# A four-layer graph network on one core: half of layer 1 by Strassen's method, its projection summed in PSUM, and some copies moved from VectorE to ScalarE

## The chip, the cores and the metric

The kernel runs on one core of a Trainium2 chip. A core has a matrix engine (TensorE, "PE" in the profile, its weight loads "PEld"), VectorE ("DVE"), ScalarE ("ACT"), GpSimd ("POOL") and SyncE ("SP"), which here issues all DMAs, in one queue and in order. The metric is the time of one execution on the device, in microseconds (us); less is better.

## The reference, cut to what matters

Four attention layers over one graph of 3327 nodes with 256 features each. Every layer adds its result to its input and normalises the sum over the features. The layer that the change touches is layer 1, a graph attention layer:

```python
h = x @ W                              # 256 -> 256
e = (h @ a[:D])[:, None] + (h @ a[D:])[None, :]
e = leaky_relu(e, 0.01)
attention = softmax(where(adj > 0, e, MASK_VAL), axis=1)
h_prime = attention @ h
x = layernorm(x + elu(h_prime))
```

Layer 0 is attention by cosine similarity, layer 2 scaled dot-product attention with learned q, k and v, and layer 3 consists of three graph attention layers like layer 1 (called 3a, 3b and 3c).

## The kernel before, in words

**Tiles and blocks.** The nodes are padded to 26 tiles of 128. The queries are taken in 7 blocks of 512 (four tiles; the last block has two tiles, 256 queries). A layer is 7 blocks by 26 steps: step (b, j) multiplies the weights of key tile j for the queries of block b with the values of tile j, and sums over j in PSUM. All of it is f32.

**One step of layer 1.** `Gat.weights` (L785) makes one tile of weights e, 128 keys by 512 queries: ScalarE computes re (L788), VectorE adds, and multiplies by the mask (L801). TensorE then multiplies e, 128 queries at a time, with V of tile j, which has 256 features and a column of ones that gives the softmax's sum: four matmuls of 257 columns (L1687). Weights are made three steps ahead in the program; the pool "e" has nine buffers, and the engines run ahead as far as buffers allow.

**Strassen's method.** Layers 0 (blocks 1 to 5), 2, 3a, 3b and 3c take a pair of key tiles and pairs of query tiles as a 2x2 by 2x2 product of blocks, in seven products in place of eight (L940: matmuls of 128 columns, or 129 with the column of ones). For that VectorE makes sums of e (L884 to L887, or L872 to L875 for four tiles of layer 3 at once). The sums of V, "tsums", are made once per pair of key tiles by `combine` (L845 to L853), stored to DRAM (L854, t_d) and fetched again for every block and pair (L858, 256.5 KB each, three buffers). Layer 1 in this kernel is plain.

**The end of a block.** `finish` (L1102) is a generator that moves on by one piece per step while the next block runs. In layer 1 it takes the reciprocal of the softmax's sums (L1198, L1201), normalises on ScalarE into p (L1186), splits p into upper and lower 16 bits ("planes", L994, ScalarE), transposes by DMA (L997, "turned"), copies the two halves to pT (L1004, VectorE), and multiplies with the layer's W. For blocks 0 to 4 this projection is done by Strassen as well, in `projected4`: sums of pT ("psums", L1043 to L1046), seven products of two matmuls each into fresh places of PSUM (L1058), one copy on ScalarE (L1071) and seven additions on VectorE (L1072 to L1082). Then come elu, the addition of x (L1258, L1267), the statistics (L1114, L1115) and the last step of the layernorm, o (L1296, VectorE); o is stored (L1308), and is split, transposed and copied once more (ft, L1004) to be projected to layer 2's values (pv, L1326, v at L1333), keys' sums (ksum, L630 to L633) and tsums.

**What sets the order.** The program is written step by step; a tile scheduler then fixes each engine's own order, in which the engine runs, waiting where its next instruction must wait. Masks (1664 KB per block of four tiles, two buffers) are fetched by `fetch_mask` (L427), u, the query side of the weights, at L775.

The functions that the diff touches:

Of the kernel before, what the change touches and what calls it, by code (L numbers as in the profile page):

```python
# [33 lines left out]
def gnn_stack(ctx: ExitStack, tc: tile.TileContext, a: dict, N: int, out: bass.AP):  # L34
# [31 lines left out]
    def bank(name):  # L66
        return ps_b.tile([P, CH], F32, tag="pb", name=name)
# [25 lines left out]
    for k in range(4):  # L93
# [18 lines left out]

    t_d = {
        k: [dram.tile([P, 4 * H + 1], F32, name=f"t{k}_d{p}") for p in range(NT // 2)]
        for k in ("0", "2", "3a", "3b", "3c")
    }
    x_d = {
        k: [dram.tile([P, D], F32, name=f"x{k}_d{t}") for t in range(NT)]
# [697 lines left out]
    def strassen(L, b):  # L816
# [3 lines left out]
            return b < NB - 1  # L820
        return L.key == "2"

    def deep(L):
        return L.i > 2

# [5 lines left out]
    def combine(key, p, v, e=None):  # L831


        b1, b2 = v[2 * p], v[2 * p + 1]
        b11, b12, b21, b22 = b1[:, H:D], b1[:, :H], b2[:, H:D], b2[:, :H]
        if (key, p) in kept or key == "0":
            t = work.tile([P, 4 * H + 1], F32, tag="tsum", name="tsums", bufs=3)
        else:
            t = work.tile([P, 4 * H + 1], F32, tag="x4k", name="tsum", bufs=2)
        if (key, p) in kept:  # L840
            tsums[kept[key, p], p] = t
        t1, t2, t3, t4 = (t[:, c : c + H] for c in (0, H + 1, 2 * H + 1, 3 * H + 1))
        if e is None:
            nc.gpsimd.memset(t[:, H : H + 1], 1.0)
            nc.vector.tensor_tensor(t1, b12, b11, ALU.subtract)  # L845
            nc.vector.tensor_tensor(t3, b22, b12, ALU.subtract)
        else:
            one = t[:, H : H + 1]
            nc.vector.tensor_scalar(one, e[:, :1], 0.0, None, ALU.is_ge)
            nc.vector.scalar_tensor_tensor(t1, b12, one, b11, ALU.mult, ALU.subtract)  # L850
            nc.vector.scalar_tensor_tensor(t3, b22, one, b12, ALU.mult, ALU.subtract)
        nc.vector.tensor_tensor(t2, b22, t1, ALU.subtract)
        nc.vector.tensor_tensor(t4, t2, b21, ALU.subtract)  # L853
        nc.sync.dma_start(t_d[key][p], t)  # L854
# [23 lines left out]
    def sums(b, e1, e2):  # L878

        hw = bw(b) // 2  # L880
        s3, s1, s2, s4 = (x[:, i, :hw] for x in two_slots("ssum") for i in range(2))
        e11, e21 = e1[:, :hw], e1[:, hw : 2 * hw]
        e12, e22 = e2[:, :hw], e2[:, hw : 2 * hw]
        nc.vector.tensor_tensor(s3, e11, e21, ALU.subtract)  # L884
        nc.vector.tensor_tensor(s1, e21, e22, ALU.add)
        nc.vector.tensor_tensor(s2, s1, e11, ALU.subtract)  # L886
        nc.vector.tensor_tensor(s4, e12, s2, ALU.subtract)  # L887
        return e11, e12, e22, s1, s2, s3, s4

    def places(pos, b):  # L890

# [95 lines left out]
    def turn(x4, n, out, steps=3, copy=nc.vector.tensor_copy):  # L987

        half = "p k (n t) -> p t k n"
        pl = work.tile([P, 4, 2, D], U16, tag="x4k", name="planes", bufs=2)
        for t in range(2):
            nc.scalar.copy(pl[:, :n, t, :], x4[:, :n, :].bitcast(U16).rearrange(half, t=2)[:, t])  # L994
        yield
        tr = work.tile([P, 16, P], U16, tag="stage", name="turned", bufs=4)
        nc.sync.dma_start_transpose(  # L997
            out=tr[:, : 4 * n, :], in_=pl[:, :n].rearrange("p k t n -> p (k t n)")
        )
        for _ in range(steps):  # L1000
            yield
        trv = tr[:, : 4 * n, :].rearrange("p (k t h) i -> p t k h i", t=2, h=2)
        for t in range(2):
            copy(out(t), trv[:, t])  # L1004
        yield

    def early(L, b):
# [17 lines left out]
    def sum_weights(wt):  # L1025
        b11, b12, b21, b22 = (wt[:, h, o * H : (o + 1) * H] for h in range(2) for o in range(2))
        t1, t2, t3, t4 = wsum
        nc.vector.tensor_tensor(t1, b12, b11, ALU.subtract)
        nc.vector.tensor_tensor(t3, b22, b12, ALU.subtract)
        nc.vector.tensor_tensor(t2, b22, t1, ALU.subtract)  # L1030
        nc.vector.tensor_tensor(t4, t2, b21, ALU.subtract)

    def projected4(pT4, wt, c4):

# [15 lines left out]
        cv = c4.rearrange("p (a k) (o f) -> p a k o f", k=2, o=2)  # L1050
        c11, c12, c21, c22 = (cv[:, :, k, o, :] for k in range(2) for o in range(2))

        def two(*pairs):

            pm = bank("pproj")
            for i, (l, r) in enumerate(pairs):
                for k in range(2):
                    nc.tensor.matmul(  # L1058
                        pm[:, (2 * i + k) * P : (2 * i + k + 1) * P],
                        l[:, k, :],  # L1060
                        r,
                        start=True,
                        stop=True,
                    )
            v = pm.rearrange("p (i a f) -> p i a f", i=2, a=2)
            return v[:, 0], v[:, 1]

        m1, m2 = two((a11, b11), (a12, b21))
        m6, m7 = two((s2, t2), (s3, t3))
        yield  # L1070
        nc.scalar.copy(c22, m1)  # L1071
        nc.vector.tensor_tensor(c11, c22, m2, add)  # L1072
        nc.vector.tensor_tensor(c22, c22, m6, add)
        nc.vector.tensor_tensor(c21, c22, m7, add)
        m5, m4 = two((s1, t1), (a22, t4))
        yield
        nc.vector.tensor_tensor(c12, c22, m5, add)
        nc.vector.tensor_tensor(c22, c21, m5, add)
        nc.vector.tensor_tensor(c21, c21, m4, sub)
        m3, _ = two((s4, b22))  # L1080
        yield
        nc.vector.tensor_tensor(c12, c12, m3, add)  # L1082

    class Sum:

# [16 lines left out]
    def finish(L, b, pos):  # L1102
# [76 lines left out]
        else:  # L1179
# [9 lines left out]
            if strassen(L, b):  # L1189
                z, L.joined = joined(pos, b, p4)  # L1190
                nc.vector.tensor_scalar(z, z, TINY, None, ALU.max)
                nc.vector.reciprocal(z, z)
                for k in range(n):
                    normed(p4[:, k, :], p4[:, k, :], z[:, k : k + 1])
            else:
                for k, t in enumerate(ts_):
                    ri = cols.tile([P, 1], F32, tag="ri", name="ri", bufs=4)
                    nc.vector.tensor_scalar(  # L1198
                        ri, pos[k][:, D : D + 1], TINY, None, ALU.max
                    )  # L1200
                    nc.vector.reciprocal(ri, ri)  # L1201
                    normed(p4[:, k, :], pos[k][:, :D], ri)
            if L.key in x_d:
                x4 = work.tile([P, 4, D], F32, tag="stage", name="x4", bufs=4)
                xr = [x4[:, k, :] for k in range(4)]
# [7 lines left out]
            if L.key != "2":  # L1213
# [5 lines left out]
                        "p k h (i t) -> p t k h i", t=2  # L1219
                    )[:, t],  # L1220
                    turn_steps(L, b),
                    nc.scalar.copy if early(L, b) else nc.vector.tensor_copy,
                )
                if early(L, b):
                    yield
                    yield
                pTs = {k: pT4[:, k] for k in range(n)}
                if L.key == "1" and b < NB - 2:
# [55 lines left out]
        if not L.hidden:  # L1284
# [7 lines left out]
                dsts = [o4[:, k, :] for k in range(n)]  # L1292
            else:
                dsts = [nxt[t][:, :D] for t in ts_]
            for k, t in enumerate(ts_):
                nc.vector.tensor_scalar(  # L1296
                    dsts[k],
                    ys[k],
                    st[:, k, 0:1],
                    r[:, k : k + 1],  # L1300
                    ALU.subtract,
                    ALU.mult,
                )
                if L.key == "3c":
                    q = LASTP if t == NT - 1 else P
                    nc.sync.dma_start(out[t * P : t * P + q, :], dsts[k][:q])
# [7 lines left out]
            if L.key == "1":  # L1314
# [4 lines left out]
                        "p h (k i t) -> p t k h i", k=4, t=2  # L1319
                    )[:, t, :n],  # L1320
                    4 if b == NB - 2 else 3,
                )
                for k, t in enumerate(ts_):
                    pm = bank("pv")
# [35 lines left out]
        if b == NB - 1:  # L1360
# [2 lines left out]
                L.sum.add(t, x)  # L1363
            yield
            L.sum.close(nxt[NT - 1])
            if L.i:
                yield
                combine(layers[L.i + 1].key, NT // 2 - 1, nxt)
            if L.gat_next is not None:
# [151 lines left out]
        return j < NT - 2 and (b > 0 or j > 3)  # L1521

    def make_weights(L, b, j, es=None):
        if strassen(L, b) and j % 2 == 0 and kept.get((L.key, j // 2)) != b:
            fetch_tsum(L.key, b, j // 2)
        if by_pairs(L, b, j // 2):
            if j % 2 == 0:
# [3 lines left out]
        else:  # L1531
            if L.is_gat:
                made.append(L.gat.weights(b, j))
                if deep(L) and strassen(L, b) and in_quad(b, j):
                    made[-1] = cells.setdefault((L.i, b, j // 2), []) if j % 2 else None
                    if j % 4 == 3:
# [54 lines left out]
    for s, (L, b, j) in enumerate(steps):  # L1591
# [6 lines left out]
        if j == 0:  # L1598
            wo, no = (CH, 4) if strassen(L, b) else (D + 1, len(tiles_of(b)))
            pos = [  # L1600
                ps_o.tile([P, wo], F32, tag="po", name="po") for _ in range(3 if end else no)
            ]
        if first:

# [42 lines left out]
        if end:  # L1647
# [33 lines left out]
                ends.append(finish_last(pos[0], xm, 0))  # L1681
            if ends:
                next(ends[0], None)
        elif not strassen(L, b):
            todo = [(es, j, k) for k in range(len(pos))]
            for e, i, k in todo:
                nc.tensor.matmul(  # L1687
                    pos[k],
                    e[:, k * P : (k + 1) * P],
                    V[L.i % 2][i],  # L1690
                    start=(i == 0),
                    stop=(i == NT - 1),
                )
        elif j % 2:
            products(pos, b, j // 2, es, V[L.i % 2], between if L.key == "2" else None)
        if s == 3:
# [29 lines left out]
        begin = 14  # L1726
        if deep(L) and b < NB - 1:
            begin = 2 if last and b == NB - 2 else 10
        if L.key == "1" and (b, j) == (0, 22):
            sum_weights(w[L.w])  # L1730
        if L.key == "2" and b * NT + j in KSTEPS:
# [96 lines left out]
```

## Time and profile before

| | us |
|---|---|
| median of 3 runs | 2264.83 (2264.76 to 2266.15) |
| profiled execution | 2266.49 |
| its span in the profile | 2264.7 |
| TensorE busy | 2235.8 |
| VectorE busy | 1973.7 |
| ScalarE busy | 1320.0 |
| layer 1: start of its first product to the first of layer 2 | 467.6 to 808.3 |

A row of a group in the profile is: line, engine, operation, out<-in, shapes, count | busy time in us, mean ns of one | idle time of the engine just ahead of them in us, and what ended most of it. A row of a stretch is start:end and length, then busy time and number of instructions for PE, PEld, DVE, ACT and POOL, the granted TensorE clock, the DMA share and GB/s. A row of a timeline is start, duration, engine, line, operation, and in brackets the idle time before it with what ended it. The granted clock is 1.00 in all stretches that are read here.

By the starts of their first matmuls the blocks of layer 1 begin at 467.6, 513.5, 565.3, 617.2, 670.2, 722.1 and 773.9 us.

### The profile page before, as it was taken

The numbers are of one execution on the slowest core, as the hardware profiler recorded it, in microseconds if no ns is written. First come the engines' busy times: TensorE is split into PE (matmuls) and PEld (weight loads), VectorE is DVE, ScalarE is ACT, GpSimd is POOL, SyncE is SP. The second block draws the span as 40 slices with busy tenths as digits, with TensorE's granted clock in tenths as the row PEclk, the third lists the DMA queues.
The fourth block names the chain that finished last, engine by engine and source line by source line (L and its number), as shares of the span: only waits on it lengthen the run. The fifth ranks groups of instructions, "written<-read, shape, count | busy, mean of one in ns | idle before, by whom it ended". The sixth has DMA issues, their size and how long they took to land. (4 is left out here: it accounts for less than half of the span.)

```text
span 2264.7 us, 42094 instructions
## 1 busy us (share of the span) xinstructions
PE 2235.8 (99%) x15333; PEld 2027.7 (90%) x15333; DVE 1973.7 (87%) x5386; ACT 1320.0 (58%) x2259; POOL 42.3 (2%) x196
## 2 busy tenths in 40 slices
PE   9999999999999999999999999999999999999997
PEld 7788887888888879999999998999999999999997
DVE  6789999967677778988998879999899999899997
ACT  4677777765545534444444445666666765665663
POOL 0000001000000000000000000000000000000000
PEclk9999999999999999999999999999999999999999
DMA  8655655522322232232232244545435545355542
GB/s 277 198 179 169 194 193 191 175 90 72 87 82 56 68 87 82 62 96 88 61 96 73 74 146 144 147 137 151 130 112 155 143 131 152 103 159 167 152 121 56
DMA packets 186210, 286.16 MB, mean 126 GB/s; under 512 B 80413, under 2 KB 105492, under 8 KB 181396
## 3 DMA queue, kind: packets, MB, share of 16 engines
q1 hardware_dynamic: 185732, 283.22, 42.3%
q8 instruction: 121, 1.98, 0.4%
q14 instruction: 85, 0.70, 0.1%
q10 hardware_dynamic: 272, 0.26, 0.0%
HBM read 228.21 MB, written 38.44 MB: 118 GB/s over the span
## 5 line engine op out<-in xcount | busy, mean ns | idle before, releaser
L788 ACT ACTIVATE re<-u,nrh,th 128x512 f32<-128x512 f32 (+1 forms) x728 | 531.8, 776 | 291.3 <-DVE e L801 146.7
L1687 PE MATMUL po<-v,e 128*128 128x257 f32 x1872 | 422.6, 381 | 1.2 <-ACT p L1186 1.1
L1687 PEld LDWEIGHTS po<-v,e 128*128 128x128 f32 x1872 | 352.6, 190 | 61.1 <-issue 9.8
L940 PE MATMUL po<-tsums,qsum 128*128 128x128 f32 (+1 forms) x2520 | 351.7, 275 | 5.8 <-DMA tsums<-t3a_d 3.0
L801 DVE SCALAR_TENSOR_TENSOR ft<-re,rh,mask 128x512 f32<-128x512 f32 x468 | 337.5, 742 | 3.2 <-ACT re L788 3.2
L940 PEld LDWEIGHTS po<-tsums,qsum 128*128 128x128 f32 x2520 | 315.4, 192 | 7.8 <-issue 2.8
L940 PE MATMUL po<-tsums,ssum 128*128 128x128 f32 (+1 forms) x2082 | 316.7, 275 | 2.1 <-DVE ssum L886 1.0
L940 PEld LDWEIGHTS po<-tsums,ssum 128*128 128x128 f32 x2082 | 286.6, 192 | 16.9 <-issue 5.0
L940 PE MATMUL po<-v,ft 128*128 128x129 f32 x1872 | 286.3, 276 | 0.9 <-DVE ft L801 0.5
L940 PEld LDWEIGHTS po<-v,ft 128*128 128x128 f32 x1872 | 251.8, 192 | 5.7 <-DVE ft L801 1.1
L940 PEld LDWEIGHTS po<-v,e 128*128 128x128 f32 x1196 | 170.2, 191 | 35.9 <-issue 23.9
L524 ACT ACTIVATE ex<-ps,rq 128x512 f32<-128x512 f32 (+1 forms) x183 | 118.9, 652 | 114.9 <-PE ps L511 111.9
L940 PE MATMUL po<-v,e 128*128 128x129 f32 x1196 | 183.3, 275 | 0.0
L801 DVE SCALAR_TENSOR_TENSOR e<-re,rh,mask 128x512 f32<-128x512 f32 (+1 forms) x234 | 148.2, 655 | 34.5 <-PE po L1687 24.3
L496 DVE SCALAR_TENSOR_TENSOR e<-ex,mask 128x512 f32<-128x512 f32 (+1 forms) x182 | 118.1, 649 | 61.9 <-ACT ex L673 30.8
L511 PE MATMUL ps<-ft 128*128 128x512 f32 (+1 forms) x364 | 166.9, 564 | 0.0
L525 DVE SCALAR_TENSOR_TENSOR e<-ex,mask 128x512 f32<-128x512 f32 (+1 forms) x183 | 116.6, 643 | 33.4 <-ACT ex L524 33.0
L940 PE MATMUL po<-tsums,ft 128*128 128x128 f32 x936 | 143.3, 275 | 0.1
L940 PE MATMUL po<-v,qsum 128*128 128x128 f32 x840 | 128.2, 275 | 0.0
L940 PEld LDWEIGHTS po<-tsums,ft 128*128 128x128 f32 x936 | 123.5, 192 | 0.4 <-ACT p L1186 0.3
L467 DVE CUSTOM_DVE_ANT_0 acc<-acc,stage 128x1024 uint16<-128x1024 uint16 (+1 forms) x168 | 108.5, 646 | 11.3 <-DMA stage<-in_adj_a 8.2
L650 PE MATMUL ps<-gsums,ksum 128*128 128x256 f32 x408 | 111.3, 380 | 0.0
(347 smaller groups left out, 3639.5 us busy)
## 6 DMA issues: line engine op xcount, KB each, us to landing
mask<-mask_d SPq DMA_DIRECT2D x30, 1664.0 KB
stage<-in_adj_a SPq DMA_DIRECT2D x78, 512.0 KB
tsums<-t_d SPq DMA_DIRECT2D x152, 256.5 KB
tsums<-t3a_d SPq DMA_DIRECT2D x77, 256.5 KB
tsums<-t3b_d SPq DMA_DIRECT2D x77, 256.5 KB
tsums<-t3c_d SPq DMA_DIRECT2D x77, 256.5 KB
mask_d<-mask SPq DMA_DIRECT2D x6, 1664.0 KB
u<-s_d SPq DMA_DIRECT2D x24, 256.0 KB
```

What stands on the lines that cost most here:

```text
L467: nc.vector.tensor_tensor(acc, acc, st[:, h * wd : (h + 1) * wd], ALU.add)
L496: nc.vector.scalar_tensor_tensor(e[:, :wd], t_[:, :wd], 0.0, mask(b, j), ALU.add, ALU.mult)
L511: nc.tensor.matmul(ps[:, :wd], FT[j // 4][:, 0, (j % 4) * P : (j % 4 + 1) * P], FT[b][:, 1, :wd], start=True, stop=True,)
L524: nc.scalar.activation(t_[:, c], ps[:, c], AF.Exp, scale=rq[:, j : j + 1])
L525: nc.vector.scalar_tensor_tensor(e[:, c], t_[:, c], 0.0, mask(b, j)[:, c], ALU.add, ALU.mult)
L650: nc.tensor.matmul(out, l, r, start=first, stop=True, skip_group_check=True)
L788: nc.scalar.activation(t_[:, :wd], self.u[b][:, :wd], AF.Relu, bias=self.nrh[:, j : j + 1], scale=self.th[:, j : j + 1],)
L801: nc.vector.scalar_tensor_tensor(e[:, :wd], t_[:, :wd], self.rh[:, j : j + 1], mask(b, j), ALU.add, ALU.mult,)
L940: nc.tensor.matmul(o, x, y, start=(p == 0 and g not in banks[:i]), stop=(p == NT // 2 - 1 and g not in banks[i + 1 :]),)
L1687: nc.tensor.matmul(pos[k], e[:, k * P : (k + 1) * P], V[L.i % 2][i], start=(i == 0), stop=(i == NT - 1),)
```

## The change

1. In layer 1, blocks 1 to 6, the first two query tiles of a block are multiplied by Strassen's method and the other two plainly; block 6, which has only two, entirely by Strassen. `half_sums` makes four 128x128 sums per pair of key tiles (L901 to L904 after the change), `half_products` the seven products, `half_joined` puts them together at the block's end (L953 to L963). Layer 1 gets tsums of its own: `combine("1", p)` for 13 pairs, seven of them during layer 0's last block, and the fetches.
2. `projected4` adds products in PSUM, by further matmuls into the same place: four copies on ScalarE and three additions on VectorE, where it was one and seven. The number of matmuls stays. For that the sign of one sum of W is turned.
3. In blocks 0 to 4 of layer 1 (`eased`) both copies to pT and one of the two copies to ft go to ScalarE, and the last step of the layernorm as well, for which VectorE makes one small array nm.

By the fixed order of each engine, the number of matmuls of 257 columns falls by 312 and that of 128 or 129 columns rises by 546; VectorE gets 356 instructions more, ScalarE 56 more, SyncE 91 more. From layer 2's start on the order is as before. A cut of the diff:

```diff
+    def half(L, b):
+        return L.key == "1" and b > 0
+    def eased(L, b):
+        return L.key == "1" and b < NB - 2
...
+    def half_sums(e1, e2):
+        x = work.tile([P, 4, P], F32, tag="e", name="hsum", bufs=9)
+        s3, s1, s2, s4 = (x[:, i, :] for i in range(4))
+        e11, e21 = e1[:, :P], e1[:, P : 2 * P]
+        e12, e22 = e2[:, :P], e2[:, P : 2 * P]
+        nc.vector.tensor_tensor(s3, e11, e21, ALU.subtract)
+        nc.vector.tensor_tensor(s1, e21, e22, ALU.add)
+        nc.vector.tensor_tensor(s2, s1, e11, ALU.subtract)
+        nc.vector.tensor_tensor(s4, e12, s2, ALU.subtract)
+        return e11, e12, e22, s1, s2, s3, s4
...
+    def half_products(pos, b, p, es, v, ks):
...
+        for k in ks:
+            g, c, n = HALF[k]
+            nc.tensor.matmul(
+                pos[g][:, c : c + n],
+                *m[k],
+                start=(p == 0 and k in (1, 7)),
+                stop=(p == NT // 2 - 1 and k in (5, 3)),
+            )
+    def half_joined(pos, c):
...
+        nc.scalar.copy(c22, m(1))
+        v = pos[-2][:, : 3 * (H + 1)].rearrange("p (s n) -> p s n", n=H + 1)
+        nc.vector.tensor_copy(z[:, :2], v[:, 0::2, H])
+        nc.vector.tensor_tensor(z[:, :1], z[:, :1], v[:, 1, H:], add)
+        nc.vector.tensor_tensor(c11, c22, m(2), add)
+        nc.vector.tensor_tensor(c22, c22, m(6), add)
+        nc.vector.tensor_tensor(c21, c22, m(7), add)
+        nc.vector.tensor_tensor(c12, c22, m(5), add)
+        nc.vector.tensor_tensor(c22, c21, m(5), add)
+        nc.vector.tensor_tensor(c21, c21, m(4), sub)
+        nc.vector.tensor_tensor(c12, c12, m(3), add)
...
         for t in range(2):
-            copy(out(t), trv[:, t])
+            (copy[t] if isinstance(copy, tuple) else copy)(out(t), trv[:, t])
...
+        pm = bank("pproj")
+        r, m2 = pm[:, :D], pm[:, D:]
+        put(r, a11, b11, first=True)
+        put(m2, a12, b21)
+        yield
+        nc.scalar.copy(c11, both(r))
+        nc.vector.tensor_tensor(c11, c11, both(m2), add)
+        put(r, s2, t2)
+        yield
+        nc.scalar.copy(c12, both(r))
+        put(r, s3, t3)
+        q = bank("pproj")[:, :D]
+        put(q, s1, t1, first=True)
+        yield
+        nc.scalar.copy(c22, both(r))
+        nc.vector.tensor_tensor(c22, c22, both(q), add)
+        put(r, a22, t4)
+        put(q, s4, b22)
+        yield
+        nc.scalar.copy(c21, both(r))
+        nc.vector.tensor_tensor(c12, c12, both(q), add)
...
+                if eased(L, b):
+                    nc.scalar.activation(
+                        dsts[k], ys[k], AF.Identity, bias=nm[:, k : k + 1], scale=r[:, k : k + 1]
+                    )
...
-        if strassen(L, b) and j % 2 == 0 and kept.get((L.key, j // 2)) != b:
+        if (strassen(L, b) or half(L, b)) and j % 2 == 0 and kept.get((L.key, j // 2)) != b:
             fetch_tsum(L.key, b, j // 2)
...
+                if half(L, b) and j % 2:
+                    made[-1] = made[-1], half_sums(made[-2], made[-1])
...
+        elif half(L, b):
+            v = V[L.i % 2]
+            if j % 2 == 0:
+                plain(pos[:-2], es, j, v, 2)
+                if j == 2:
+                    half_products(pos, b, 0, held, v, (7, 6, 4, 3))
+            else:
+                plain(pos[:-2], es[0], j, v, 2)
+                held = es[1]
+                half_products(pos, b, j // 2, held, v, (1, 2, 5) if j == 1 else (1, 2, 5, 7, 6, 4, 3))
...
+        if L.key == "0" and b == NB - 1 and j % 3 == 0 and 0 < j < 22:
+            combine("1", j // 3 - 1, V[1])
+        if L.key == "1" and b == 0 and j % 3 == 1 and j < 15:
+            combine("1", 7 + j // 3, V[1])
```

## The prediction

> **What bounds the kernel now.** I read the busy shares first, then the groups, then the stretches, then single stretches of VectorE and SyncE. From the page:
>
> ```profile
> span 2264.7 us, 42094 instructions
> PE 2235.8 (99%) x15333; PEld 2027.7 (90%) x15333; DVE 1973.7 (87%) x5386; ACT 1320.0 (58%) x2259; POOL 42.3 (2%) x196
> L1687 PE MATMUL po<-v,e 128*128 128x257 f32 x1872 | 422.6, 381 | 1.2 <-ACT p L1186 1.1
> L940 PE MATMUL po<-tsums,ssum 128*128 128x128 f32 (+1 forms) x2082 | 316.7, 275 | 2.1 <-DVE ssum L886 1.0
> ```
>
> TensorE (PE) is busy nearly all the time. Its busy time is per row modelled, so I price a matmul by what is spent per record: 422.6/1872 = 226 ns for a 128x257 record of layer 1; in the trace such records start 217 ns apart, and the 128x128 and 128x129 records of layer 0 start 112 ns apart. An f32 matmul is two records: 434 and 224 ns. "1.2 <-ACT" says that the plain matmuls wait for nothing worth naming: layer 1 is bound by PE.
>
> Next the stretches (columns: start:end, length, then busy time and count of PE, weight loads, VectorE (DVE), ScalarE (ACT), GpSimd, then granted clock, DMA share, GB/s):
>
> ```profile
> 300.00:460.00 160.00, 159.57 (x1025) 130.78 (x1024) 149.93 (x447) 118.37 (x191) 10.18 (x27) 1.00 0.55 174
> 512.50:564.00 51.50, 51.50 (x252) 45.28 (x251) 37.60 (x100) 27.24 (x40) 1.23 (x2) 1.00 0.29 75
> 564.00:615.00 51.00, 51.00 (x249) 44.83 (x249) 35.72 (x93) 26.84 (x40) 0.77 (x2) 1.00 0.33 88
> 615.00:666.00 51.00, 49.93 (x244) 43.85 (x244) 37.87 (x102) 26.84 (x40) 1.31 (x2) 1.00 0.29 84
> 666.00:718.00 52.00, 52.00 (x255) 45.70 (x254) 37.71 (x97) 27.11 (x41) 1.32 (x2) 1.00 0.23 61
> ```
>
> The first row is layer 0, where Strassen runs already: VectorE is at 94% and PE still doesn't starve. The others are about one block of layer 1 each (51.9 us by the starts of the blocks). VectorE has 37 us of work in 52, but it doesn't rest at will: it is an in-order engine, and its idle time is made of two waits per block. This is the first of them:
>
> ```profile
> 565.74 0.17 DVE L1201 RECIPROCAL ri<-ri 128x1 f32<-128x1 f32 x1
> 575.51 1.38 DVE L1004 COPY pT<-turned 128x1024 uint16<-128x1024 uint16 x2 [9.61 <-DMA turned<-planes]
> ...
> 579.13 3.40 DVE L801 SCALAR_TENSOR_TENSOR e<-re,rh,mask 128x512 f32<-128x512 f32 x5
> ```
>
> All of VectorE stands for 9.61 us (7.5 in the other blocks) while ScalarE normalises and splits, and the DMA transposes. It costs nothing today: the weights e are up to eight tiles ahead. The second wait, ahead of the ft copies, is 2.6 to 4.2 us.
>
> **PE's part of the change.** For two key tiles, two query tiles cost 4 x 434 = 1736 ns plainly and 7 x 224 = 1568 by Strassen. 168 ns for each of 13 pairs, in 6 blocks: 13.1 us less, 2.18 per block. The projection's 14 matmuls stay.
>
> The Trainium skill, "TensorE: Matmul & The Clock Gate", section "Back-to-back issue gap", speaks against the change: it has sustained spacings of 81 ns at 128 columns and 131 at 512, the narrow matmul paying for its weight load. If 257 columns cost what lies between (some 98), 14 narrow passes would cost more than 8 wide ones, and PE would lose. The trace's 112 against 217 decides: here narrow ones are nearly in proportion.
>
> **VectorE's part, per block.** Added: four 128x128 sums per pair, L901 to L904. The same operations for ksum (L630 to L633) start 0.20 to 0.26 apart, 0.89 for four, so 13 x 0.89 = 11.6 us. The joining of seven products, seven adds of 0.25 and four small ones of 0.15, less four small ones for two tiles that need no reciprocal of their own (0.18 each): +1.7. Moved away: two pT copies (1.38 together), one ft copy (0.66), four layernorm steps (0.32 each, 1.3), four of seven projection adds (0.45 each, 1.8), against a small nm (0.15): -5.0. Net +8.3: 37.2 + 8.3 = 45.5 us for blocks 2 to 5, against 49.7 of PE. By work alone VectorE fits, at 92%.
>
> ScalarE gets two copies of the 1.35 us kind (its pT copies in layer 3 take that), a copy of ft, four steps of 0.4 and some small ones, 7 us on 27 of 52: no bound, but a link in the chain below.
>
> **The waits, which the work hides.** In the changed kernel's static order I counted what VectorE can do inside each wait.
> 1. From the last join (L963) the way is: normalise two tiles (0.8), planes (2.0: "567.01 1.99" before), transpose (4.4 alone; 6.5 from the end of planes to the copy at 575.5), two copies, now on ScalarE, one after the other (2.6), then psums on VectorE: 9.8 to 11.9. Between them VectorE's queue holds three e (0.66), half sums and ksum, 4.2 us. The wait is 5.6 to 7.7; I take 6.0. It stands ahead of e of tile 9, which everything later queues behind.
> 2. SyncE's queue. Before, the transpose of o went out ahead of the fetch of the next mask; now the order is tsums, mask (which waits for VectorE's e of tile 25), then that transpose. The trace of before has this order once:
>
> ```profile
> 798.16 0.32 SPq L427 DMA_DIRECT2D mask<-mask_d  x1
> 798.71 7.03 SPq L997 DMA_TRANSPOSE turned<-planes  x1
> ```
>
> and the copy of that transpose starts at 807.78: 9.6 us after the mask's issue. VectorE has five half sums, e of four tiles, two more groups of half sums, the small ones and e of tile 4 to do meanwhile, 7.0 us. The wait is 2.6 us; it would be 0 if the transpose took its lone 5 us. The 7.03 us that SyncE is held also delay three tsums fetches of the next block.
>
> The cycle of VectorE is thus 45.5 + 6.0 + 2.6 = 54.1 us, against 51.9 before and the 49.7 that PE would allow. The cover has shrunk too: e and half sums share nine buffers, three per pair, so the lead is six tiles instead of nine, and a wait of 6 us is no longer swallowed whole.
>
> **The sum**, against the profiled execution (2266.5, of which 2264.7 span; the median of the runs is 1.7 below it). Blocks 2 to 5: three at +2.2, one +0.6 since its mask is half as large: +7. Block 1 has half sums but starts with a lead from block 0, and PE's 2.2 less shows: -2. Block 6 isn't eased, and has 256 queries: a pair costs VectorE two e of 0.41 and 0.89, 1.7 us, against 1.57 of PE; with the same join and waits 38 to 40 us for 34.3: +4.5. Layer 0's last block gets the sums of V for layer 1 (12 of the 13 combines, by VectorE's fixed order; 0.83 each, 10 us) where VectorE has about 10 us free between 425 and 467: 0 to 3, I take +1.5. At layer 2's start, V of the last tiles comes later by the longer chain: +1.5. 13 t_d stores and 78 fetches of 256.5 KB: the DMA share in these stretches is 0.23 to 0.33 and layer 0 runs at 0.55, nothing. Sum +12.5: 2279 profiled, 2277 as a median.
>
> Both ends: waits at 7.7 and 4 with block 6 at 42 give +22, or 2287. With the first wait at 4 and the second gone, each block is PE's or nearly so.
>
> **Rivals.**
> - *Faster.* VectorE keeps up as at 94% in layer 0, for the waits fall inside the lead: its cycle is below 49.7 if the two together are under 4.2 us. Then the five four-tile blocks gain 2.2 each, 11 in all, and block 6 and layer 0 give back 1 to 3: 2266.5 - 9 = 2257.5, 2256 as a median, at best 2252. For it speaks the row of layer 0, where VectorE has waits too and PE none; against it the 9.61 and the order of SyncE.
>
> The Trainium skill is on this side: "Perfetto Trace Analysis", section "Identifying the Most-Contended Engine", ranks engines by occupancy, and by that PE at 49.7 stays ahead of VectorE at 45.5 and the change would bring its whole 13 us. The 9.61 us in which VectorE stood with work behind it is why I don't count it so.
> - *No change.* The waits together are 4.2 to 7, the cycle 50 to 52.5: blocks 1 to 5 gain 0 to 5, block 6, layer 0 and layer 2's start take it back: 2261 to 2269.
> - *It doesn't do what it says.* Excluded for PE: the listing has 312 fewer wide and 546 more narrow matmuls, 135.4 - 122.3 = 13.1 us.
>
> **Numbers.** Forecast, VectorE's chain bounds layer 1: 0.60, 2270 to 2288, likeliest 2277. Faster: 0.27, around 2256. No change: 0.13. The range reaches down into the faster rival, 2254, and up to 2287. 0.2%, about what a measurement of this kernel tells from no change, is 4.5 us: the bounds are 2260.3 and 2269.4.
>
> **What would show it.** Right: in blocks 2 to 5 gaps of PE of 2 to 4 us per block put down to hsum (L903, L904) or e, block starts 53 to 55 us apart, a VectorE gap of some 6 us ahead of psums L1119 and one of 2 to 4 ahead of ft L1080, SyncE held at the transpose behind the mask. Wrong: no gaps of PE above 0.5 us and blocks of 49.7, with VectorE's idle only before buffers of e. Layers 2 to 3c must be unchanged to 1 us, since their instructions keep their order. I would be wrong if the transpose passes the mask, if the half sums are cheaper than 0.89, or if the lead at the block's end is more than I count.

## The result and the profile after

| | us |
|---|---|
| before, median of 4 runs | 2264.97 (2264.76 to 2266.15) |
| changed, median of 4 runs | 2286.11 (2282.14 to 2289.16) |
| ratio | 1.0093, 95% interval 1.008 to 1.0105 |
| profiled execution of the changed kernel, its span | 2289.16, 2287.2 |

The change costs 21 us. 2277 was forecast. The page of the changed kernel:

```profile
span 2287.2 us, 43671 instructions
PE 2234.1 (98%) x15801; PEld 2036.5 (89%) x15801; DVE 2026.0 (89%) x5742; ACT 1359.6 (59%) x2315; POOL 41.9 (2%) x209
L914 PE MATMUL po<-v,e 128*128 128x257 f32 x1248 | 295.3, 381 | 0.6 <-DVE e L525 0.4
```

The plain group has lost its third (1872 to 1248 records), and TensorE's total is hardly lower, 2235.8 to 2234.1: a matmul's busy time lasts longer where the clock is low, and that hides part of what was saved. The stretches of layer 1 tell more (columns as before: PE, PEld, DVE, ACT, POOL, clock, DMA share, GB/s):

```profile
564.00:615.00 51.00, 47.77 (x302) 43.54 (x303) 41.44 (x138) 31.64 (x46) 0.70 (x2) 0.97 0.43 125
615.00:666.00 51.00, 47.29 (x311) 43.20 (x311) 41.54 (x143) 31.84 (x48) 0.77 (x2) 1.00 0.51 127
666.00:718.00 52.00, 46.09 (x282) 41.38 (x281) 38.01 (x127) 28.36 (x42) 0.76 (x2) 0.93 0.49 121
```

Before, TensorE was idle in none of these but one; now it is for 3 to 6 us of each. VectorE is at 73 to 81%, so it isn't simply full. And the granted clock is below 1 in two of the three. What TensorE waited for in layer 1 (TensorE's waits from 468 to 829 us: total, times, longest):

```profile
PE pv L1428 <- ACT ft L1080: 10.7, 4, 3.4
PE pproj L1131 <- ACT pT L1080: 6.1, 4, 2.6
PE po L937 <- DMA tsums<-t_d: 3.4, 2, 2.8
PE po L937 <- DVE pT L1080: 1.6, 1, 1.6
PE pproj L1131 <- DVE c L1149: 1.2, 1, 1.2
PE po L937 <- DVE hsum L903: 0.5, 1, 0.5
```

The same view of before has two rows, 1.1 and 0.7 us. Of the new ones, the half sums have half a microsecond. TensorE waits at the finish's own matmuls: at pv, for the ft copy, and at the projection, for the pT copies, both now on ScalarE. The largest case, in TensorE's timeline:

```profile
672.95 1.47 PE L914 MATMUL po<-v,e 128*128 128x257 f32 x6
677.59 6.67 PE L1428 MATMUL pv<-w_l_wvt,ft 128*128 128x256 f32 x16 [3.17 <-ACT ft L1080]
```

3.17 us of standing still, and then 16 records in 6.67 us, 417 ns each, where such records start 216 ns apart at full clock. The clock says why; these two stretches end where it changed:

```profile
673.35:676.76 3.41, 1.07 (x5) 0.58 (x4) 0.56 (x1) 0.78 (x2) 0.45 (x1) 1.00 1.13 304
676.76:683.59 6.83, 6.00 (x14) 4.84 (x15) 4.66 (x20) 1.59 (x2) 0.22 (x1) 0.50 0.06 23
```

And on SyncE's queue, ahead of that wait:

```profile
664.64 0.32 SPq L427 DMA_DIRECT2D mask<-mask_d  x1
665.67 7.68 SPq L1073 DMA_TRANSPOSE turned<-planes  x1
673.47 1.76 SPq L864 DMA_DIRECT2D tsums<-t_d  x3
```

The transpose is held behind the mask for 7.68 us, and the three tsums of the next block behind the transpose. VectorE's two waits are there too:

```profile
676.20 0.74 DVE L1080 COPY ft<-turned 128x1024 uint16<-128x1024 uint16 x1 [3.15 <-DMA turned<-planes]
698.73 0.43 DVE L1119 TENSOR_TENSOR psums<-pT 128x256 f32<-128x256 f32 x1 [6.87 <-ACT pT L1080]
```

But VectorE also waits for TensorE, to write e where TensorE has still to read (VectorE's waits from 468 to 829 us):

```profile
DVE e L801 <- PE po L914: 11.1, 13, 1.4
DVE e L801 <- PE po L937: 5.0, 10, 1.5
```

**An account of layer 1**, worked out from the starts of TensorE's records between layer 1's first matmul and layer 2's first product: the sum of the full-clock spacings (217, 112 or 216 ns by width), then every excess of over 0.25 us as a wait, then the smaller excesses, among them what the low clock costs.

| kernel (profiled execution) | length | at full clock | waits | smaller excesses |
|---|---|---|---|---|
| before | 340.7 | 337.6 | 2.3 | 0.8 |
| changed | 360.6 | 324.5 | 27.3 | 8.9 |

(The profiled execution of the changed kernel is the slowest of its four.) 13.1 us are saved, to the tenth; 25.0 of waits and 8.1 of smaller excesses are added. Of the latter the low clock has at most 6.8: TensorE had half the clock for 13.7 us of layer 1 (567.53 to 570.95, 676.76 to 683.59, 734.79 to 738.20). 19.9 of the 22.5 us between the spans are this, 1.2 come before layer 1 and 1.2 after layer 2's start.

### The profile page after: what moved, and what is told of

Its sections match the earlier page's. It is cut to its first block, busy times and chain, and to the rows that moved or that the text cites. A ratio compares the mean times of both kernels' runs of the same rounds, so it can differ in the third digit from the quotient of the medians.

```text
span 2287.2 us, 43671 instructions
## 1 busy us (share of the span) xinstructions
PE 2234.1 (98%) x15801; PEld 2036.5 (89%) x15801; DVE 2026.0 (89%) x5742; ACT 1359.6 (59%) x2315; POOL 41.9 (2%) x209
## 5 line engine op out<-in xcount | busy, mean ns | idle before, releaser
L914 PE MATMUL po<-v,e 128*128 128x257 f32 x1248 | 295.3, 381 | 0.6 <-DVE e L525 0.4
L914 PEld LDWEIGHTS po<-v,e 128*128 128x128 f32 x1248 | 229.3, 190 | 40.2 <-issue 7.9
L1016 PEld LDWEIGHTS po<-v,e 128*128 128x128 f32 x1196 | 170.2, 191 | 36.1 <-issue 23.4
L801 DVE SCALAR_TENSOR_TENSOR e<-re,rh,mask 128x512 f32<-128x512 f32 (+1 forms) x234 | 151.2, 655 | 28.7 <-PE po L914 11.1
L496 DVE SCALAR_TENSOR_TENSOR e<-ex,mask 128x512 f32<-128x512 f32 (+1 forms) x182 | 118.1, 649 | 54.9 <-ACT ex L673 30.3
L467 DVE CUSTOM_DVE_ANT_0 acc<-acc,stage 128x1024 uint16<-128x1024 uint16 (+1 forms) x168 | 108.3, 645 | 12.7 <-DMA stage<-in_adj_a 10.9
```

The costliest lines, as they stand in the source:

```text
L467: nc.vector.tensor_tensor(acc, acc, st[:, h * wd : (h + 1) * wd], ALU.add)
L496: nc.vector.scalar_tensor_tensor(e[:, :wd], t_[:, :wd], 0.0, mask(b, j), ALU.add, ALU.mult)
L801: nc.vector.scalar_tensor_tensor(e[:, :wd], t_[:, :wd], self.rh[:, j : j + 1], mask(b, j), ALU.add, ALU.mult,)
L914: nc.tensor.matmul(pos[k - k0], e[:, k * P : (k + 1) * P], v[i], start=(i == 0), stop=(i == NT - 1),)
L1016: nc.tensor.matmul(o, x, y, start=(p == 0 and g not in banks[:i]), stop=(p == NT // 2 - 1 and g not in banks[i + 1 :]),)
```

## The experiments

All times are medians of runs beside runs of the kernel before on the same chip (2264.4 to 2265.8); differences are against that. Theory A: SyncE's order (mask ahead of the transpose) and the waits behind it. Theory B: VectorE has too much work. Theory C, formed after the third run: the moves to ScalarE and the sums in PSUM cost by themselves.

| run | us | against before | ratio, 95% |
|---|---|---|---|
| changed kernel | 2286.1 | +21.1 | 1.008 to 1.0105 |
| 1 mask behind the transpose | 2276.4 | +10.9 | 1.0028 to 1.0059 |
| 2 one half sum of four | 2282.3 | +16.8 | 1.0054 to 1.0087 |
| 3 plain, with the moves and PSUM | 2289.2 | +23.7 | 1.0079 to 1.0125 |
| 4 block 6 plain | 2295.1 | +29.6 | 1.0116 to 1.0161 |
| 5 Strassen's half alone | 2268.8 | +3.6 | 1.0009 to 1.0028 |
| 6 half, and PSUM | 2269.1 | +3.9 | 1.0009 to 1.0028 |
| 7 PSUM alone | 2282.7 | +17.5 | 1.0066 to 1.0096 |
| 8 the moves alone | 2279.1 | +13.8 | 1.0048 to 1.0082 |
| 9 mask behind, pT back on VectorE | 2273.1 | +8.7 | 1.0023 to 1.0049 |
| 10 half, PSUM, projection later | 2268.0 | +3.6 | 1.0004 to 1.0022 |
| 11 half alone, pT and ft later | 2271.1 | +6.7 | 1.0017 to 1.0042 |
| 12 as 10, one half sum of four | 2262.8 | -3.0 | 0.9978 to 0.9997 |

**1. The mask behind the transpose.**

```diff
-            masks[nb] = fetch_mask(nb)
+            if L.key == "1" and ft_turned[0] is not None:
+                with tc.issue_after(ft_turned[0].ins):
+                    masks[nb] = fetch_mask(nb)
```

> The changed kernel, with one difference: in layer 1 the fetch of the next mask is queued on SyncE behind the transpose of o that ends in ft, where the changed kernel has it ahead. Theory A (SyncE's order): the changed kernel's 1.7 to 3.6 us gaps of TensorE ahead of pv, one per block, come from that transpose being behind 1.66 MB of mask, and so does the lowered clock after them; here they fall below 1 us and the time by 10 to 15 us, to 2270 to 2276. Theory B (VectorE has too much work in a block, wherever the mask stands): the gaps move to hsum, and the time stays within 4 us of the changed kernel's 2286.

10 us come back, as A has it: half of the loss. TensorE's waits at pv shrink from 10.7 to

```profile
PE pv L1432 <- ACT ft L1083: 4.1, 3, 2.3
PE pproj L1134 <- DVE c L1152: 3.7, 4, 1.3
PE pproj L1134 <- ACT pT L1083: 2.4, 2, 2.2
```

with 2.2 and 0.6 in two further rows for pv. They don't fall below 1 us each, which A had expected; that the copies on ScalarE hold them up here too is a reading, not tried in this run. B isn't supported; hsum has 0.6 us.

**2. One half sum of four.**

```diff
-        nc.vector.tensor_tensor(s3, e11, e21, ALU.subtract)
         nc.vector.tensor_tensor(s1, e21, e22, ALU.add)
-        nc.vector.tensor_tensor(s2, s1, e11, ALU.subtract)
-        nc.vector.tensor_tensor(s4, e12, s2, ALU.subtract)
-        return e11, e12, e22, s1, s2, s3, s4
+        return e11, e12, e22, s1, s1, s1, s1
```

> The changed kernel with three of the four half sums per pair left out (only s1 = e21 + e22 is made, and it stands for the other three in the products, so layer 1's result is another): 8.7 us less work for VectorE per block, the same matmuls. Theory B (VectorE's work is the cause): the time falls below the kernel before, to 2250 to 2256, with no gap of TensorE left in layer 1. Theory A (SyncE's order): gaps ahead of pv of 1 to 3 us stay in blocks where the mask still goes ahead of the transpose, and only block 6 and part of the rest is won: 2262 to 2272.

4 us for 52 us less work of VectorE (8.7 in each of six blocks), far from the 2250 to 2256 of B; A's 2262 to 2272 was too low as well. The waits at pv fall (10.7 to 7.1 us), those at the projection for pT stay (6.1 and 6.9). The 4 us understate what the cut does in layer 1: in the profiled executions it takes 349.6 us in place of 360.6, and 5 of these 11 us are lost behind it, since TensorE waits 4.7 us for the first tsums of layer 2, which SyncE holds behind a transpose (6.61 us) behind the mask. So VectorE's work has a part in the changed kernel's loss, but B falls as its main cause.

**3. Plain matmuls, with the moves and the sums in PSUM.**

```diff
     def half(L, b):
-        return L.key == "1" and b > 0
+        return False
```

(and no sums of V for layer 1)

> Layer 1 by plain matmuls throughout, as before, but with the projection summed in PSUM and with the copies and the layernorm step on ScalarE. Theory A: the mask goes ahead of the transpose of o here too, but VectorE has 32 us of work per block and its lead hides the wait: 2263 to 2268, with ft copied later than before. A third theory, that the move to ScalarE alone costs (its 1.35 us copies, one after the other, make TensorE wait at the projection): over 2270.

The surprise of the study: without any Strassen in layer 1 the kernel is as slow as with it, or slower. Theory A's 2263 to 2268 is refuted here; that the moves cost is not yet separated from the sums in PSUM. Its four middle blocks against the changed kernel's and those of before (564 to 771 us; first run 3, then the changed kernel, then the kernel before):

```profile
564.00:771.00 207.00, 194.04 (x910) 169.03 (x909) 119.31 (x323) 121.59 (x180) 2.25 (x6) 0.96 0.26 64
```

```profile
564.00:771.00 207.00, 190.72 (x1205) 173.43 (x1206) 162.05 (x539) 124.80 (x182) 3.00 (x8) 0.97 0.47 123
```

```profile
564.00:771.00 207.00, 205.93 (x1002) 180.97 (x1002) 148.56 (x392) 105.83 (x159) 4.70 (x8) 1.00 0.28 77
```

VectorE has 119 us of work in 207, 29 less than in the kernel before (in which TensorE did 10% more records in this time), and TensorE stands still for 13. A kernel can lose its time with an engine relieved: here what the engine did early is done later by another. The waits are elsewhere than in the changed kernel:

```profile
PE pproj L1131 <- DVE c L1149: 13.0, 5, 3.4
PE pproj L1332 <- DVE pT L1080: 2.1, 1, 2.1
PE pv L1428 <- ACT ft L1080: 1.6, 3, 0.7
```

**4. Block 6 plain.**

```diff
-        return L.key == "1" and b > 0
+        return L.key == "1" and 0 < b < NB - 1
```

> The changed kernel with block 6 of layer 1, which has two query tiles, by plain matmuls. It prices the last block alone, where 1.7 us of VectorE per pair stand against 1.57 of TensorE: theory B' (VectorE's rate bounds that block) has it back at 34 to 36 us from 41.5, and the time at 2279 to 2281; if the block is long only because of a late start of VectorE, less than 3 us come back.

9 us slower than the changed kernel, where 5 to 7 faster was expected. By the account layer 1 is 2.7 us shorter (357.9), but block 6 isn't: from its first product to layer 2's it takes 43.0 us where the changed kernel takes 41.6. So its length isn't what the rate of VectorE would make of it. The rest of the run, from layer 2's first product, takes 1454.0 us against 1444.8, with more small gaps in layer 3, though the order of the instructions there is the changed kernel's. That isn't explained.

**5 to 8, the parts one by one.** Run 5 has `projected4` of before and

```diff
     def eased(L, b):
-        return L.key == "1" and b < NB - 2
+        return False
```

Run 6 has only the latter. Run 7 is run 6 with `half` false; run 8 is the changed kernel with `half` false and `projected4` of before.

> Strassen's half of layer 1 alone: the projection as before (one copy, seven additions on VectorE), and all copies and the layernorm step on VectorE as before. SyncE's order is mask behind the transpose of o again. If the loss of the changed kernel comes from the moves to ScalarE and from the sums in PSUM (theory C, formed after the plain kernel with the moves took 2289), it goes here: TensorE's gaps ahead of pproj and pv are below 1 us each and the time is 2255 to 2268, held up from 2253 only by VectorE, which has 50 us of work per block. If VectorE's work is the cause after all (theory B), it has 5 us more of it per block than in the changed kernel, and the time is 2290 or more.

> Strassen's half and the projection summed in PSUM, but pT, ft and the layernorm step on VectorE as before. By theory C with the sums in PSUM as a cause of its own (the second product into a PSUM place waits until ScalarE has copied the first one out, and that copy stands behind re in ScalarE's queue) it is 3 to 8 us above the run with Strassen's half alone, with gaps at the projection's later matmuls; if only the copies matter, the two are within 2 us.

> The kernel before with the projection summed in PSUM as the only difference. If TensorE's wait for ScalarE's copies between two sums in PSUM is a cause: gaps of 1 to 3 us per block at the projection, 2270 to 2282. If not: 2264 to 2267.

> The kernel before with the copies of pT, one copy of ft and the last layernorm step on ScalarE as the only difference (VectorE makes nm). If ScalarE's slower copies are a cause: gaps of TensorE ahead of the projection's first matmuls (they wait for psums, which wait for pT), 1 to 3 us per block, and 2270 to 2285. If only the sums in PSUM are: 2264 to 2267.

Strassen's half alone costs 3.6 us, just above what C allowed, and its waits at pv didn't fall below 1 us each, as C had it (8.0 us in six, the longest 2.0). The two other parts cost 17.5 and 13.8 without it; for run 7 that is 0.7 us above the top of what was expected. They don't add: together 23.7, and beside Strassen's half the sums in PSUM cost nothing that can be told (run 6 against 5, where the expectation had 3 to 8). For run 7 the place can be read. TensorE's timeline, then ScalarE's, then VectorE's, all of run 7:

```profile
587.81 1.22 PE L1131 MATMUL pproj<-ft,psums 128*128 128x128 f32 x4 [3.77 <-DVE c L1149]
```

```profile
583.12 0.81 ACT L788 ACTIVATE re<-u,nrh,th 128x512 f32<-128x512 f32 x1 [11.13 <-DVE e L801]
584.12 2.93 ACT L788 ACTIVATE re<-u,nrh,th 128x512 f32<-128x512 f32 x4 [0.19 <-DVE e L801]
586.95 0.35 ACT L1148 COPY c<-pproj 128x256 f32<-128x256 f32 x1
```

```profile
579.74 1.36 DVE L1080 COPY pT<-turned 128x1024 uint16<-128x1024 uint16 x2 [11.10 <-DMA turned<-planes]
587.33 0.42 DVE L1149 TENSOR_TENSOR c<-c,pproj 128x256 f32<-128x256 f32 x1 [0.60 <-ACT c L1148]
```

From right to left: VectorE stands for 11.10 us at pT. So e isn't made, the buffers of re are full, and ScalarE stands too (11.13). When both move again, five re go first, and only then ScalarE's copy of the first product; VectorE's addition waits for it, and TensorE for the addition, since its next product goes into the same bank of PSUM: into the half that the copy reads, beside the half that the addition reads. In the kernel before that product went into another bank, and TensorE has no such wait there. VectorE's waits at pT are no longer in run 7 than before (42.6 us in six, 42.5 in seven). Of TensorE's waits in run 7, 9.0 us in five are at this one place.

In run 8 they are at the ft copy, that stands behind the mask as in the changed kernel:

```profile
PE pv L1423 <- ACT ft L1080: 7.5, 4, 3.0
PE po L914 <- ACT p L1262: 1.7, 2, 1.2
PE pproj L1134 <- ACT pT L1080: 0.9, 1, 0.9
```

The gaps were expected at the projection, with psums; they are at pv.

By the fixed orders, the mask goes ahead of the transpose of o in runs 3, 7 and 8 as in the changed kernel, and behind it in 5 and 6 as in the kernel before. So it is not the half that turned the order round; and what runs 7 and 8 show for each part alone holds this order too, which no run with plain matmuls puts back. With Strassen's half the parts can be told apart step by step: half alone +3.6 (run 5), with the sums in PSUM +3.9 (run 6), with the moves as well and the mask still behind +10.9 (run 1), with the mask ahead +21.1 (the changed kernel). So of the 21 us the half has 3.6, the sums 0.3, the moves 7.0 and the mask's place 10.2, each to some 3 us.

**9. The mask behind, and pT back on VectorE.** Run 1's edit, and

```diff
-                    nc.scalar.copy if early(L, b) or eased(L, b) else nc.vector.tensor_copy,
+                    nc.scalar.copy if early(L, b) else nc.vector.tensor_copy,
```

> The changed kernel with two differences: the mask fetch behind the transpose of o (as in the run with only that, 2276) and the two pT copies back on VectorE. One ft copy, the layernorm step and the sums in PSUM stay as changed. If ScalarE's pT copies are the other part of the loss (2.6 us one after the other, against 1.4 on VectorE), gaps ahead of the projection fall below 1 us and the time is 2264 to 2270; if they are not, it stays within 3 us of 2276.

Against the kernel before it is +8.7 for +10.9 in run 1: 2.2 us come back, and the second expectation holds. With the mask behind, the pT copies are a small part. The largest wait now is the PSUM one (`pproj <- DVE c`, 5.1 us in five).

**10 and 11. The finish later in TensorE's order.** Runs 6 and 5 with the mask behind and

```diff
-            return 5 if b == NB - 2 else 3
+            return 5 if b == NB - 2 else 4 if b < NB - 2 else 3
```

and in run 11 one step more ahead of the ft copy too.

> Strassen's half and the sums in PSUM, copies on VectorE, mask behind the transpose, and the copies to pT (so the projection and all behind it) one step later in the program. The run without the later step has TensorE wait 1 us per block at the projection for pT, 1 us at the block's start and 2 at layer 2's start, some 13 us in all, which eat the 13 us that Strassen saves. If the waits are a matter of where the matmuls of the finish stand in TensorE's order, they go and the time is 2258 to 2265; if VectorE's 49 us of work per block is the bound, the waits move elsewhere and it stays at 2267 to 2272.

> Strassen's half alone (the projection as before), mask behind the transpose, the copies to pT and to ft one step later each in the program. The run without the later steps has gaps of 1.1 us at the projection and 0.6 to 2.1 us at pv per block. If their place in TensorE's order is the cause: 2258 to 2265. If VectorE's work is: 2267 to 2272.

Neither gains anything: both times lie in the range that was given for waits that move elsewhere. Run 10 is +3.6 where run 6 is +3.9, which can't be told apart; run 11 is +6.7 where run 5 is +3.6. In run 10 the waits for pT at layer 1's projection (3.3 us in run 6) are gone and others take their place (`pproj <- DVE c` 4.0, `po <- DVE p` 2.6, `pproj <- DVE pT` at layer 2's start 2.2). No kernel with the whole computation that came out of the change is nearer to the kernel before than runs 5 and 10, at +3.6.

**12. Run 10 with one half sum of four** (the edit of run 2).

> The run with Strassen's half, the sums in PSUM and the later projection (copies on VectorE, mask behind the transpose; 2268), with three of the four half sums per pair left out, so that layer 1's result is another: 8.7 us less for VectorE per block. In the changed kernel the same cut brought 4 us only. If what holds this version above the 2252 that TensorE's saving allows is VectorE's work, the time falls to 2250 to 2258; if it is the chain of transposes, copies and waits also here, it stays above 2262.

6.6 us against run 10 (+3.6 to -3.0) for 52 less of VectorE, and 3 us below the kernel before; 2262.8 is far from 2250 to 2258 and just above the 2262 of the other reading. In time that is more than the 4 of run 2, in layer 1 it is less (341.3 to 338.7, where run 2 has 360.6 to 349.6); either way the full saving isn't reached. The account for this and the other kernels:

| profiled execution of | length | at full clock | waits | smaller excesses |
|---|---|---|---|---|
| 1 mask behind | 348.5 | 324.5 | 17.3 | 6.7 |
| 3 plain, moves and PSUM | 366.7 | 337.6 | 19.5 | 9.6 |
| 5 half alone | 344.3 | 324.5 | 15.8 | 4.1 |
| 7 PSUM alone | 357.0 | 337.6 | 16.7 | 2.7 |
| 8 moves alone | 353.1 | 337.6 | 13.1 | 2.4 |
| 10 half, PSUM, later | 341.3 | 324.5 | 13.1 | 3.7 |
| 12 as 10, one half sum | 338.7 | 324.5 | 10.6 | 3.6 |

Run 10 had the full clock in all of layer 1, so its 3.7 us of smaller excesses are no low clock. In every kernel with Strassen's half in this table TensorE has its 13.1 us; in each, 10 to 27 us of waits at pT, ft, p, c and tsums take them, and neither undoing the other parts (run 5) nor moving the finish (run 10) nor relieving VectorE (run 12) brings them to the 2.3 of the kernel before.

## Why the prediction was right, and where it was not

The direction and the range held; the likeliest time was 9 us too low, and the mechanism is half of the one that was told. That 2286.1 came to lie inside the range, 1 us below its end, is in part luck: a part of the 21 us comes from costs that the sum doesn't hold.

- *TensorE saves 13.1 us.* Right: 337.6 to 324.5 at full clock. The narrow matmul does cost half of the wide one.
- *VectorE's two waits, 6.0 and 2.6 us.* Right, with SyncE held at the transpose: 6.9 and 3.2 in the block shown, 6.7 and 2.3 in the next. Run 1 shows that the mask's place is worth 10 us.
- *"The cycle of VectorE is thus 45.5 + 6.0 + 2.6 = 54.1 us."* This step failed. It made VectorE the engine that bounds layer 1 and let its waits reach TensorE through hsum, in gaps of 2 to 4 us per block. The waits at hsum were 0.5 us in all. VectorE was busy for 162 of 207 us, it waited 16 us in layer 1 for TensorE itself (11.1 and 5.0), and taking 52 us of work off it in six blocks made layer 1 only 11 us shorter, of the 36 that it lies above its time at full clock, and the kernel 4 us faster (run 2). The waits reach TensorE directly: pv and the projection stand in its own order, and when ft or pT is late everything behind them is. From block 2's first product (562.37) to block 6's (787.82) a block took 56.4 us. That 54.1 is near is in part luck: the same transposes stand behind both, but the length is TensorE's own time, 4.2 us per block of waits at pv and the projection, and the low clock.
- *"ScalarE gets two copies of the 1.35 us kind ... no bound, but a link in the chain below."* A link, and the price was left out: the moves cost 7.0 us beside the half (run 1 against run 6), and 13.8 alone, with the mask ahead (run 8). I asked what the move frees on VectorE, and not how much later the copy's reader starts.
- *"four of seven projection adds (0.45 each, 1.8)"*, counted as pure gain. It brought none: run 6 can't be told from run 5, and the sums in PSUM alone, with the mask ahead, cost 17.5 us (run 7). The step added a wait of TensorE for a read of PSUM by another engine, and nothing was priced for that.
- *The clock.* Not in the sum at all: up to 6.8 us, of the 10 by which the profiled execution (2289) lies above the 2279 of the sum.
- *"+22, or 2287."* The upper end doesn't follow from its own terms: with waits of 7.7 and 4 the cycle is 57.2, 5.3 above the blocks of before, and with block 6 at 42 and the other terms kept the sum is about +28, or 2293.
- *Block 6 at 38 to 40 us, by VectorE's rate.* The waits there were for a tsums DMA (2.8 us of them in one), for pT and only 0.5 for hsum; in run 4, by plain matmuls, the block took 43.0 us against 41.6. Not supported. The tsums fetches, priced at nothing, make TensorE wait 3.4 us, for they queue behind the held transpose; with the mask behind (run 1) no such wait is left.
- *Layer 0's end and layer 2's start, 1.5 each.* 1.2 at the end of layer 0; at layer 2's start pv waits 2.0 where it was 0.5. Right.
- *The rival "faster"* needed the two waits together under 4.2 us; they were 8.5 in the mean (30.3 and 12.1 us in five). The rule of the Trainium skill that spoke for it ("Perfetto Trace Analysis", "Identifying the Most-Contended Engine": the engine with the highest occupancy is the most contended) names TensorE in layer 1 (in the 207 us above, weight loads for 173.4 and matmuls for 190.7, against 162.1 of VectorE), and by the waits TensorE was indeed the engine to watch; but it doesn't say what a change brings. In run 3 VectorE is at 58%, and that kernel is the second slowest that was run.

What stays open: why the sums in PSUM cost 17.5 us by themselves and nothing beside Strassen's half, and what run 4 loses behind layer 2's start. For the first there are two readings, neither tried: the late copy of run 7 comes from five re in a row, where in run 6 VectorE waits at pT for 21.6 us in place of 42.6 and e and re are more spread out; and run 7 has the mask ahead of the transpose, run 6 behind it.

## What to carry to other kernels

Ask of every edit first which instruction of the bound engine's own queue reads its result, and how much later that result comes; what is freed on an engine that isn't the bound comes after. Summing in PSUM saves additions but can make the next matmul wait for the reader of the last; a copy on a free but slower engine delays its reader by the difference and by what stands ahead of it in that engine's queue. And try the parts of a change one by one: here the part that looked costly took 3.6 us, and the two that were to pay for it cost 0.3 and 7.0 more beside it, and 17.5 and 13.8 alone. And look at what a part does to the fixed order: the mask's place, which no line of the change asks for, took 10 us.

## What the runs showed of the hardware

- TensorE's waits cost a second time, through its clock. In layer 1 of the changed kernel it was granted at half from 567.53, 676.76 and 734.79 us, for 3.4, 6.8 and 3.4 us. These starts lie 109.2 and 58.0 us apart, 32 and 17 times 3.413 us, so the trace can be cut into stretches of 3.41 us that end where a half begins. The first pair of rows is around the first start, the second pair around the wait of 2.82 us that ends at 791.25:

```profile
564.12:567.53 3.41, 1.12 (x5) 1.02 (x6) 2.17 (x8) 2.51 (x3) 0.61 (x1) 1.00 0.85 250
567.53:570.95 3.42, 3.42 (x10) 2.69 (x9) 2.07 (x8) 0.20 (x1) 0.00 (x0) 0.50 0.00 0
789.40:792.81 3.41, 1.56 (x9) 1.49 (x10) 2.29 (x10) 1.93 (x2) 0.67 (x1) 1.00 0.76 227
792.81:796.22 3.41, 3.41 (x21) 3.10 (x21) 3.31 (x13) 0.00 (x0) 0.00 (x0) 1.00 0.00 0
```

  TensorE was busy for 1.12, 1.07 and 1.35 us of the stretches ahead of the three halves, and for 1.56 us of the one after which the clock stayed at 1.00. So the length of a wait alone doesn't decide: the one of 2.56 us ahead of pv at 733.44 was followed by half the clock, and the one of 2.82 us, of which 1 us falls into the stretch before, was not. No exact limit can be read: ahead of a half at 1434.52 the row has 1.76 us busy, with ends that are modelled. The Trainium skill, "TensorE: Matmul & The Clock Gate", section "What's actually happening", has the clock at half after an idle window of about 3.4 us that runs freely. The half, the length and the free running agree; but a third of the window was busy here each time, so the window need not be wholly idle.
- The changed kernel's time and its mean clock go together: 2282.1 us at 0.997, 2283.4 at 0.996, 2288.8 at 0.995 and 2289.2 at 0.994; 0.003 of 2287 us is 6.9, the whole distance between the ends (an estimate, since only one of the four was profiled). It isn't the only cause of scatter: the ten runs of run 10 lie between 2264.0 and 2271.7 at 0.998 and 0.997.
- A DMA transpose issued just behind a 1.66 MB fetch held SyncE's queue for 5.0 to 8.9 us in five blocks, and its result was copied 8.1 to 11.6 us after the fetch's issue (9.6 had been read from the one case of before). With the fetch behind it (run 1) the same transpose held the queue for 2.0 to 3.4 us.
